# A layer of triangle multiplication and spectral convolution: the last tile's column sums by matmul, the product's bias on GpSimd

## The chip, the cores and the metric

The kernel runs on one core of a Trainium2 chip. The metric is device time in microseconds, from the start to the end of one execution; the median of three executions before the change is 1853.18 us (1850.88 to 1853.84).

Engines are named as in the profile: PE (TensorE, matmuls; PEld is its loading of weights), DVE (VectorE), ACT (ScalarE), POOL (GpSimd), SP (SyncE, which here only issues transfers). SBUF is the working memory of 128 partitions, PSUM the memory that PE writes to; POOL doesn't read PSUM in this kernel.

## What is computed

The input x is 512 x 512 positions of 64 channels, float32. Layer 0 is a gated triangle product, layer 1 a convolution in the spectral domain, each behind a group norm and added to its input. Cut to what matters:

```python
xn = _ln(x, norm_w, norm_b)                       # x is already group-normed
left  = (xn @ left_w + left_b) * mask * sigmoid(xn @ lgate_w + lgate_b)
right = (xn @ right_w + right_b) * mask * sigmoid(xn @ rgate_w + rgate_b)
out_gate = sigmoid(xn @ ogate_w + ogate_b)
out = einsum('bkjd,bkid->bijd', left, right)
out = _ln(out, onorm_w, onorm_b) @ out_w + out_b
x1 = x + out * out_gate                           # layer 0

x_ft = fft2(_gn(x1))[:, :, :12, :12]              # layer 1
out_ft = einsum('bcmn,comn->bomn', x_ft, w_real + 1j * w_imag)
x2 = x1 + real(ifft2(out_ft, padded with zeros))
```

Only 12 x 12 frequencies are kept, so that both transforms are matmuls with small tables of cosines and sines. The mask is 0 or 1 for each of the 512 rows and columns; positions whose row or column is masked out get `out_b` for the product.

## The kernel before

Rows and columns are ranked by the mask, so that those that count come first. With at most 256 of them the function `compact` runs, and it does in these executions. Its stages, with the times of the profile: statistics of x and the compact copy (to 90 us), the projections left and right (to 400 us), the products of the 64 channels (to 666 us), the rows of the product (to 815 us), the units of layer 0's output (to 1515 us), and layer 1's small transforms and the last pass (to the end).

From 666 to 1515 us one loop runs over steps s (line 1096 on), under a manual schedule: instructions stand on each engine in the order of the program, and nothing is reordered. A step is 8 positions of each of the 128 partitions; 8 steps make a tile k of 64. The first 8 tiles (`first`) are the product, held in `places`; then come 32 units v = k - 8, each a pair of 32-column tiles of x for half of the rows. `last` is unit 31. In step (k, n) PE transposes step s + 13 (`t_ps`, line 957, `LEAD` = 13), multiplies step s + 12 for its centered values (`y_ps` for the product, whose second half is already the output projection, `c_ps` for x), and ACT squares these and copies; DVE adds up the squares (L1000), ACT takes the square root (L1006) once for a tile, DVE the reciprocal of it (L1164), and DVE then multiplies the projection by that factor (L1170) into `z_t`, 16 positions in two steps, and adds a bias (L1173) that lies in PSUM (`bias_ps`, part of `scratch`). In the product `z_t` goes to DRAM as `u_d`, from SP. `z_t` has four buffers, `xt_c` 15.

In the units z becomes the output gate by a sigmoid on ACT (L1124); POOL multiplies it by the product's rows that `load_u` brought from `u_d`, or by the bias row where the row is masked (`gated`, L1026), and adds it to x in place (`added`, L1030). The result is stored to `x_h` by SP (`store`), measured for the group norm by DVE (L1075), and reduced over rows by PE into `f_ps` (`transform`, L1057), 24 sums for each of 32 columns. `save` copies `f_ps` to `ft` and writes it to DRAM, `modes_d`, one row for each of the 512 columns. A quarter of these, 128 columns, is brought back with columns as partitions (`fetch`) and summed over columns by 12 matmuls (`column_sums`, L891), which DVE adds to `sums` (L894). The first three quarters are summed inside the loop (`columns`, at the units 11, 19 and 27). The last needs the last unit: after the loop `fetch(3)` runs on POOL's queue, behind `memset` of `picks`, and its matmuls stand among the steps of the group norm's affine (`group_norm_affine`, whose argument `between` is called after its two matmuls).

`sums` are then turned (L1227), scaled into `picks`, multiplied by the weights (`mixed_ps`, L1245), and transformed back for the first columns (`back_columns`). The last pass takes 64 tiles of 128 rows and 32 columns (1024 KB each): four matmuls (`l_ps`, L1309), four adds on DVE (L1316), a store to the output. These tiles are gathers from `x_h` on POOL (`fetch_rows`, line 914), in rank order, with 15 buffers (`AHEAD`): two are fetched inside the loop, at step n = 3 of the last two units, 11 after `fetch(3)`, two into `picks` when the mixing is done, and each of the others when a tile has left its buffer. `load` (line 1008) brings the units' x tiles, also by gathers on POOL, and is called at n = 3 and 6 three units ahead. Everything on POOL, gathers too, keeps its order.

`places` is one SBUF tensor of eight parts (`place(i)`): the product, then x of five units at a time (`x_of`: parts 0, 1, 3, 4, 2), `u` in parts 5 and 6, `modes_t` and `ft` in part 7, and at the end the weights from part 3 on.

Of the kernel before, what the change touches and what calls it, by code (L numbers as in the profile page):

```python
# [9 lines left out]
F32 = mybir.dt.float32  # L10
# [36 lines left out]
def conv_preact_kernel(ctx: ExitStack, tc: tile.TileContext, t: dict):  # L47
# [193 lines left out]
    def group_norm_affine(keep, sets, each, name, between=lambda i: None):  # L241
# [5 lines left out]
        with tc.tile_pool(name="gn_" + name, bufs=1) as gp, tc.tile_pool(  # L247
# [6 lines left out]
            between(0)  # L254
# [12 lines left out]
            between(1)  # L267
# [346 lines left out]
    def compact(fc):  # L614
# [193 lines left out]
        with tc.tile_pool(name="tri", bufs=1) as trp:  # L808
# [57 lines left out]
            with tc.manual_schedule(), tc.tile_pool(name="late", bufs=1) as lp:  # L866
# [4 lines left out]
                nc.scalar.dma_start(turn, t["c_turn"])  # L871
                sums = lp.tile([P, MODES, M2], F32, name="sums")
# [12 lines left out]
                def column_sums(h, pool):  # L885

                    by = modes_t.rearrange("p (m k) c -> p m (k c)", k=2)
                    ps = pool.tile([P, 4, P], F32, name="t_ps").rearrange("p i k -> p (i k)")[:, : MODES * M2]
                    ps = ps.rearrange("p (m n) -> p m n", m=MODES)
                    steps = [  # L890
                        lambda m=m: nc.tensor.matmul(ps[:, m, :], by[:, m, :], col_basis[:, h, :], start=True, stop=True)  # L891
                        for m in range(MODES)
                    ]
                    return steps + [lambda: nc.vector.tensor_add(sums, sums, ps)]  # L894

                def columns(h, pool):
                    for step in column_sums(h, pool):
                        step()

                def fetch(h):  # L900

                    (nc.gpsimd if h == 3 else nc.sync).dma_start(modes_t, modes_d[h * P : (h + 1) * P])
# [4 lines left out]
                buffers = [places[:, free : free + JC * C].rearrange("p (n c) -> p n c", c=C)]  # L907
                buffers += [place(i)[:, r * JC : (r + 1) * JC] for i in (6, 2, 0, 1) for r in range(2)]
                buffers += [place(7)[:, JC:]]
# [8 lines left out]

                with tc.tile_pool(name="np_x", bufs=LEAD + 2) as tp, tc.tile_pool(
# [5 lines left out]
                ) as s1, tc.tile_pool(name="np_t", bufs=2, space=PSUM) as ps_t, tc.tile_pool(  # L925
                    name="np_n", bufs=1, space=PSUM
                ) as ps_n, tc.tile_pool(name="opf", bufs=1, space=PSUM) as ps_f, ExitStack() as products:
# [14 lines left out]
                    totals = [scratch[:, i, : SIZE * 8] for i in range(2)]  # L942
                    eps = lp.tile([P, 1], F32, name="eps")
# [119 lines left out]
                    def save(jc):  # L1063
                        ft = places[:, 7 * 64 * C + M2 * C : 7 * 64 * C + 32 * C].rearrange("p (j c) -> p j c", c=C)
                        nc.scalar.copy(ft.rearrange("p j c -> p (j c)"), fs.pop(jc))
                        for g in range(4):
                            o = jc * JC + 8 * g
                            queue = nc.scalar if jc == NJ - 1 else nc.sync
                            queue.dma_start(modes_d[o : o + 8].rearrange("j m c -> m j c"), ft[32 * g : 32 * g + M2])
# [29 lines left out]
                    for s in range(-LEAD, total_g + 2 * SIZE):  # L1099
# [49 lines left out]
                        if (v, n) in ((last - 1, 3), (last, 3)):  # L1149
                            fetch_rows(len(fetched))  # L1150

# [11 lines left out]
                        if n == 7 and k + 1 in rss:  # L1163
                            nc.vector.reciprocal(rss[k + 1], rss[k + 1])  # L1164
                        if wps is not None:
# [3 lines left out]
                            rs = rss[k][:, 8 * n : 8 * n + 8].unsqueeze(2).to_broadcast([P, 8, C])  # L1169
                            nc.vector.tensor_mul(z[:, 8 * odd : 8 * odd + 8, :], wps, rs)  # L1170
                            if odd:
                                bias = bias_ps["out" if k < first else "ogate"]
                                nc.vector.tensor_add(z, z, bias.unsqueeze(1).to_broadcast([P, 16, C]))  # L1173
# [21 lines left out]
                        if n == 6 and v % 8 == 3 and 8 < v < len(units):  # L1195
                            columns(v // 8 - 1, ps_t)
                        if v == last - 1 and n == 3:
# [3 lines left out]
                with tc.tile_pool(name="lq", bufs=1) as qp, tc.tile_pool(name="lx", bufs=1) as xp:  # L1201

                    picks = qp.tile([P, MODES, MODES, 32], F32, name="picks")
                    nc.gpsimd.memset(picks, 0.0)
                    fetch(3)
                    buffers += [xp.tile([P, JC, C], F32, name=f"lx_t{i}") for i in range(AHEAD - 2 - len(buffers))]
                    spare = picks.rearrange("p m n k -> p (m n k)")
                    buffers += [spare[:, i * JC * C : (i + 1) * JC * C].rearrange("p (n c) -> p n c", c=C) for i in range(2)]
# [6 lines left out]
                    with tc.tile_pool(name="tcp", bufs=1, space=PSUM) as tcp:  # L1215
                        steps = column_sums(3, tcp)

                        def some(i):
                            for step in steps[7 * i : 7 * i + 7 - 2 * i]:
                                step()  # L1220

                        ab2 = group_norm_affine(lp, sets, 8, "x1c", some)
                        steps[-1]()
                    with tc.tile_pool(name="sps", bufs=1, space=PSUM) as sps:

                        turned = sps.tile([P, MODES, M2], F32, name="turned")
                        nc.tensor.matmul(  # L1227
                            turned.rearrange("p m n -> p (m n)"), turn, sums.rearrange("p m n -> p (m n)"), start=True, stop=True
                        )
# [28 lines left out]


# [137 lines left out]
```

## Time and profile before

The profiled execution took 1856.55 us, its span of instructions is 1854.8 us; both lie near the three of the median.

| stretch, us | PE | DVE | ACT | POOL | clock | GB/s |
|---|---|---|---|---|---|---|
| whole span, share | 89% | 78% | 51% | 47% | 0.89 | 252 |
| product, 690 to 785 (95 us) | 88 | 91 | 79 | 3 | 0.96 | 167 |
| units, 900 to 1000 (100 us) | 97 | 98 | 74 | 96 | 0.98 | 262 |
| 1500 to 1550 (50 us) | 23 | 30 | 4 | 29 | 0.59 | 352 |
| last pass, 1600 to 1700 (100 us) | 91 | 69 | 12 | 20 | 0.50 | 426 |

The numbers of the engines are busy microseconds of the stretch. The clock is the share of full speed that PE was granted. [...] GB/s is what the transfers moved. In the groups of instructions, a row gives line, engine, operation, tile written and read, shapes and count, then busy time, mean of one in ns, and the idle time of the engine just before them with what ended it. PE's float32 matmuls leave two records each. In the chain of waits, a row is a start, a length and the engine and line that held the end at that time; the letters q stand for the queue of an engine that issues a transfer.

### The profile page before, as it was taken

The page shows a single profiled execution, that of the slowest core. Times are in us where ns is not written, and L with a number is a line of the kernel's source. Part 1 is how long each engine was busy: PE and PEld are TensorE (multiplying, and loading weights), DVE is VectorE, ACT ScalarE, POOL GpSimd, SP SyncE. Part 2 cuts the span into 40 slices and gives each one's busy share as a digit, 9 for nine tenths or more (in the row PEclk, how much of TensorE's full clock was granted, in tenths as well). Part 3 has the DMA queues.
Part 4 walks back from the last instruction along what each step waited for, and adds up shares of the span by engine and source line. Part 5 has one row for each costly group of instructions (what it writes and reads, how often), then busy time and mean ns, then how long its engine had stood idle before and what let it go on. Part 6 is the DMA issues. An engine that isn't in the chain of part 4 may idle for free.

```text
span 1854.8 us, 33850 instructions
## 1 busy us (share of the span) xinstructions
PE 1644.3 (89%) x11598; PEld 1295.3 (70%) x11598; DVE 1455.1 (78%) x3001; ACT 952.9 (51%) x1670; POOL 873.7 (47%) x678
## 2 busy tenths in 40 slices
PE   6779899999899999989999999999999957998772
PEld 5666666664688777788888888888888736665441
DVE  5989677777455559999999999999999984665552
ACT  3555555554222268877777767777777720111000
POOL 3666111111000000039999999999999882112110
PEclk9989899999899999999999999999999966555555
DMA  6999255556655525347767776687676598999998
GB/s 250 383 384 374 83 130 138 139 140 159 202 181 181 177 100 199 137 159 249 259 236 244 264 272 215 230 306 248 232 264 242 197 275 357 408 426 426 426 427 378
DMA packets 188869, 468.23 MB, mean 252 GB/s; under 512 B 35184, under 2 KB 134384, under 8 KB 147600
## 3 DMA queue, kind: packets, MB, share of 16 engines
q1 hardware_dynamic: 158192, 262.40, 41.7%
q0 software_dynamic: 27856, 202.19, 28.5%
q8 instruction: 94, 1.54, 0.3%
q10 hardware_dynamic: 2640, 1.38, 0.3%
q14 instruction: 87, 0.71, 0.1%
HBM read 278.13 MB, written 187.76 MB: 251 GB/s over the span
## 4 chain that ended last, share of the span: by engine, by line
PE 23%; DVE 22%; DMA 8%; POOL 5%; issue 3%; ACT 2%; SPq 1%; DVEq 0%; ACTq 0%; POOLq 0%
DVE scratch L1000 5%; DVE z_t L1170 5%; DVE z_t L1173 5%; PE w_ps L967 5%; PE l_ps L1309 5%; PE c_ps L967 5%; DVE stats2c L1075 4%; DMA places<-x_h,dst_i 4%; POOL z_t L1026 3%; PE t_ps L957 3%; DMA out_x<-places 2%; PE f_ps L1057 2%; POOL places L1030 2%; PE y_ps L978 1%; DMA picks<-x_h,dst_i 1%
## 5 line engine op out<-in xcount | busy, mean ns | idle before, releaser
L967 PE MATMUL w_ps<-gate_x,xt_c 128*128 128x128 f32 x2048 | 282.7, 282 | 31.1 <-DVE z_t L1170 29.5
L1030 POOL TENSOR_TENSOR places<-places,z_t 128x1024 f32<-128x1024 f32 x127 | 302.2, 2379 | 8.1
L967 PEld LDWEIGHTS w_ps<-gate_x,xt_c 128*128 128x128 f32 x2048 | 254.4, 195 | 47.5 <-DVE z_t L1170 45.6
L967 PE MATMUL c_ps<-center_x,xt_c 128*128 128x128 f32 x2048 | 277.9, 279 | 6.1 <-ACT xt_c L962 5.5
L967 PEld LDWEIGHTS c_ps<-center_x,xt_c 128*128 128x128 f32 x2048 | 253.5, 195 | 9.8 <-ACT xt_c L962 8.2
L1309 PE MATMUL l_ps<-places,rinv 24*128 24x512 f32 x512 | 206.7, 1128 | 29.2 <-DVE places L1316 18.0
L1075 DVE BATCH_NORM_STATS2 stats2c<-places 128x6 f32<-128x128 f32 x1024 | 220.4, 278 | 8.2 <-POOL places L1030 8.2
L1000 DVE TENSOR_REDUCE scratch<-sq_c 128x16 f32<-128x1024 f32 x160 | 194.5, 1216 | 21.7 <-ACT sq_c L995 7.6
L1124 ACT ACTIVATE z_t<-z_t 128x1024 f32<-128x1024 f32 x128 | 135.5, 1058 | 141.9 <-DVE z_t L1173 126.3
L1173 DVE TENSOR_TENSOR z_t<-z_t,scratch 128x1024 f32<-128x1024 f32 x160 | 195.3, 1221 | 11.6 <-ACT rs_n L1006 3.8
L957 PE MATMUL t_ps<-c_ident,places 128*128 128x128 f32 x1280 | 200.4, 280 | 1.3 <-DVE places L855 1.3
L1309 PEld LDWEIGHTS l_ps<-places,rinv 24*128 24x128 f32 x512 | 120.9, 304 | 110.0 <-DVE places L1316 54.1
L1026 POOL TENSOR_TENSOR z_t<-z_t,bias_row_out 128x1024 f32<-128x1024 f32 x63 | 149.6, 2374 | 100.0 <-ACT z_t L1124 99.7
L957 PEld LDWEIGHTS t_ps<-c_ident,places 128*128 128x128 f32 x1280 | 145.6, 142 | 60.7 <-issue 51.5
L630 POOL DMA_INDIRECT places<-in_x,src_i x64 | 62.6, 978 | 258.5 <-PE t_ps L957 246.9
L962 ACT ACTIVATE xt_c<-t_ps,ab_xc 128x512 f32<-128x512 f32 x256 | 175.9, 687 | 15.5 <-PE t_ps L957 10.2
L1170 DVE TENSOR_TENSOR z_t<-w_ps,rs_n 128x512 f32<-128x512 f32 x256 | 171.8, 672 | 5.3 <-PE w_ps L967 5.3
L1316 DVE TENSOR_TENSOR places<-places,l_ps 128x512 f32<-128x512 f32 x176 | 109.3, 682 | 79.3 <-PE l_ps L1309 39.8
L992 ACT ACTIVATE sq_c<-c_ps 128x512 f32<-128x512 f32 x256 | 150.5, 588 | 31.0 <-PE c_ps L967 30.7
L680 DVE BATCH_NORM_STATS2 stats1c<-x_ps 128x6 f32<-128x512 f32 x256 | 155.7, 680 | 12.4 <-PE x_ps L679 12.0
L1026 POOL TENSOR_TENSOR z_t<-z_t,places 128x1024 f32<-128x1024 f32 x64 | 151.5, 2367 | 15.1 <-ACT z_t L1124 15.0
L665 ACT COPY xc<-xg 128x128 f32 x352 | 105.0, 298 | 68.3 <-POOL xc L665 32.5
(208 smaller groups left out, 2614.7 us busy)
## 6 DMA issues: line engine op xcount, KB each, us to landing
x_h<-places SPq DMA_DIRECT2D x64, 1024.0 KB
out_x<-places SPq DMA_DIRECT2D x44, 1024.0 KB
places<-u_d SPq DMA_DIRECT2D x512, 64.0 KB
left_d<-o_c SPq DMA_DIRECT2D x64, 256.0 KB
right_d<-o_c SPq DMA_DIRECT2D x64, 256.0 KB
left_raw<-left_d SPq DMA_DIRECT2D x64, 256.0 KB
right_raw<-right_d SPq DMA_DIRECT2D x64, 256.0 KB
u_d<-z_t SPq DMA_DIRECT2D x32, 512.0 KB
```

Source lines behind the costliest of these rows:

```text
L680: nc.vector.bn_stats(stats[:, 0, 16 * (jc % quarter) + 4 * r + c, :], ps.rearrange("p i k -> p (i k)"))
L957: nc.tensor.transpose(tps[:, i, :], flat[:, o : o + P], ident)
L962: nc.scalar.activation(xts[s], tps, AF.Identity, bias=ab1[:, 2:3])
L967: nc.tensor.matmul(ps[:, 2 * i : 2 * i + 2, :], xts[s][:, i, :], w, start=True, stop=True)
L992: nc.scalar.activation(sq, cps, AF.Square)
L1000: nc.vector.tensor_reduce(totals[k % 2][:, 8 * (n - 1) : 8 * (n + 1)], sqs.pop(s // 2), AX.X, ALU.add)
L1026: nc.gpsimd.tensor_mul(zs[k, c], zs[k, c], u)
L1030: nc.gpsimd.tensor_add(xr, xr, zs.pop((k, c)))
L1075: nc.vector.bn_stats(st[k // 4][:, g, k % 4, :], x_of(k)[:, :, 2 * g : 2 * g + 2])
L1170: nc.vector.tensor_mul(z[:, 8 * odd : 8 * odd + 8, :], wps, rs)
L1173: nc.vector.tensor_add(z, z, bias.unsqueeze(1).to_broadcast([P, 16, C]))
L1309: nc.tensor.matmul(ps.rearrange("p j o -> p (j o)"), rinv[h, b, :], it[h], start=True, stop=True, tile_position=(32 * g, 0),)
```

## The change

Four things are changed.

1. In the product the bias of `z_t` is added by POOL from the row in SBUF, and no longer by DVE. The units keep theirs on DVE.
2. In the product the reciprocal is written to two halves of `scratch` in PSUM (`factors`), and the multiplication reads it there. DVE's inputs are then one from SBUF and one from PSUM.
3. The last quarter of the columns is split. Its first 96 columns are fetched at (last, 5) from ACT's queue and multiplied at (last, 7) into `t_ps`, 12 matmuls that start an accumulation. The last 32 columns don't go through DRAM: 16 matmuls multiply `ft`, as it stands in SBUF, by `spread_e` and add to the same `t_ps`. `spread_e` holds the cosines and sines of these 32 columns, spread over 12 x 24 places so that each row of `ft` reaches its own; ACT builds it in 24 instructions of 192 elements from two new constants (`last_basis`, `last_mask`) in steps 2 to 5 of the last unit, in a part of `places` that the last `u` has left. `sums` takes `t_ps` between the variance's matmul and the root, where `turned` is now issued too.
4. The order of the last pass's buffers is changed, and one gather more is issued in the loop (at (last - 2, 3)) and one directly after it, ahead of the `memset`.

On POOL the six gathers of the first three units, which were its first instructions in this stage, now stand among the adds of the product: the first after 21 of them, the others two adds apart.

```diff
-    def group_norm_affine(keep, sets, each, name, between=lambda i: None):
+    def group_norm_affine(keep, sets, each, name, between=lambda: None):
...
             nc.tensor.matmul(mean_ps, avg, part, start=True, stop=True)
-            between(0)
...
             nc.tensor.matmul(var_ps, avg, v, start=True, stop=True)
-            between(1)
+            between()
...
+                last_basis = lp.tile([P, 8, M2], F32, name="last_basis")
+                nc.scalar.dma_start(last_basis, t["c_last_basis"])
+                last_mask = lp.tile([P, M2], F32, name="last_mask")
+                nc.scalar.dma_start(last_mask, t["c_last_mask"])
...
+                def columns(h, pool):
+                    q = P if h < 3 else P - JC
...
+                    for m in range(MODES):
+                        nc.tensor.matmul(ps[:, m, :], by[:q, m, :], col_basis[:q, h, :], start=h < 3 or m == 0, stop=h < 3)
+                    if h < 3:
+                        nc.vector.tensor_add(sums, sums, ps)
+                    return ps
...
-                    (nc.gpsimd if h == 3 else nc.sync).dma_start(modes_t, modes_d[h * P : (h + 1) * P])
+                    q = P if h < 3 else P - JC
+                    (nc.scalar if h == 3 else nc.sync).dma_start(modes_t[:q], modes_d[h * P : h * P + q])
+                spread_e = places[:, 7 * 64 * C - 8 * 2 * MODES * M2 : 7 * 64 * C]
+                spread_e = spread_e.rearrange("p (j k m n) -> p j k m n", j=8, k=2, m=MODES)
+                def prepare(some):
+                    for i in some:
+                        nc.scalar.mul(spread_e[:, :, i // MODES, i % MODES, :], last_basis, last_mask[:, i : i + 1])
...
-                buffers = [places[:, free : free + JC * C].rearrange("p (n c) -> p n c", c=C)]
-                buffers += [place(i)[:, r * JC : (r + 1) * JC] for i in (6, 2, 0, 1) for r in range(2)]
-                buffers += [place(7)[:, JC:]]
+                buffers = [place(7)[:, JC:], places[:, free : free + JC * C].rearrange("p (n c) -> p n c", c=C)]
+                buffers += [place(2)[:, r * JC : (r + 1) * JC] for r in range(2)]
...
+                    factors = [scratch[:, i, SIZE * 8 :] for i in range(2)]
...
                         nc.scalar.copy(ft.rearrange("p j c -> p (j c)"), fs.pop(jc))
+                        if jc == NJ - 1:
+                            ps = ends[0].rearrange("p m n -> p (m n)")
+                            for j in range(8):
+                                for k in range(2):
+                                    e = spread_e[:, j, k].rearrange("p m n -> p (m n)")
+                                    nc.tensor.matmul(
+                                        ps[k * C : (k + 1) * C], ft[:, j, :], e,
+                                        start=False, stop=(j == 7), tile_position=(0, k * C),
+                                    )
+                            return
...
-                        if (v, n) in ((last - 1, 3), (last, 3)):
+                        if (v, n) in ((last - 2, 3), (last - 1, 3), (last, 3)):
                             fetch_rows(len(fetched))
+                        if v == last and 2 <= n < 6:
+                            prepare(range(6 * n - 12, 6 * n - 6))
...
-                            nc.vector.reciprocal(rss[k + 1], rss[k + 1])
+                            nc.vector.reciprocal(factors[(k + 1) % 2] if k + 1 < first else rss[k + 1], rss[k + 1])
...
-                            rs = rss[k][:, 8 * n : 8 * n + 8].unsqueeze(2).to_broadcast([P, 8, C])
+                            rs = (factors[k % 2] if k < first else rss[k])[:, 8 * n : 8 * n + 8]
+                            rs = rs.unsqueeze(2).to_broadcast([P, 8, C])
...
-                                bias = bias_ps["out" if k < first else "ogate"]
-                                nc.vector.tensor_add(z, z, bias.unsqueeze(1).to_broadcast([P, 16, C]))
+                                if k < first:
+                                    bias = rows_of["out"].unsqueeze(1).to_broadcast([P, 16, C])
+                                    nc.gpsimd.tensor_add(z, z, bias)
+                                else:
+                                    nc.vector.tensor_add(z, z, bias_ps["ogate"].unsqueeze(1).to_broadcast([P, 16, C]))
...
+                        if (v, n) == (last, 5):
+                            fetch(3)
+                        if (v, n) == (last, 7):
+                            ends.append(columns(3, ps_t))
...
+                    fetch_rows(len(fetched))
                     nc.gpsimd.memset(picks, 0.0)
-                    fetch(3)
...
-                        def some(i):
-                            for step in steps[7 * i : 7 * i + 7 - 2 * i]:
-                                step()
-                        ab2 = group_norm_affine(lp, sets, 8, "x1c", some)
-                        steps[-1]()
...
+                        def turn_sums():
+                            nc.vector.tensor_add(sums, sums, ends[0])
+                            nc.tensor.matmul(
+                                turned.rearrange("p m n -> p (m n)"), turn, sums.rearrange("p m n -> p (m n)"),
+                                start=True, stop=True,
+                            )
+                        ab2 = group_norm_affine(lp, sets, 8, "x1c", turn_sums)
```

## The prediction

> **What bounds the kernel now.** I read the 40 slices first, then the groups of instructions by shape inside the stages that the change touches, then the busy time in chosen stretches, and last the chain of waits from 1500 us on. Three stages matter: the product (666 to 815 us), the units (815 to 1515 us), and the end. In the groups between 700 and 780 us (columns: line, engine, operation, tile, shapes, count, busy us, mean ns, idle before):
>
> ```profile
> L978 PE MATMUL y_ps<-both,xt_y 64*128 64x128 f32 x670 | 50.7, 293 | 6.9 <-ACT xt_y L960 6.9
> L1170 DVE TENSOR_TENSOR z_t<-xt_c,rs_n 128x512 f32<-128x512 f32 x41 | 26.4, 675 | 0.0
> L1000 DVE TENSOR_REDUCE scratch<-sq_c 128x16 f32<-128x1024 f32 x21 | 25.8, 1228 | 2.2
> L1173 DVE TENSOR_TENSOR z_t<-z_t,scratch 128x1024 f32<-128x1024 f32 x21 | 25.6, 1221 | 1.1
> L1164 DVE RECIPROCAL rs_n<-rs_n 128x64 f32<-128x64 f32 x6 | 3.3, 544 | 0.0
> ```
>
> DVE's four groups sum to 81 us, while busy overlaps a little, in 80 us: DVE is the bound of the product. It takes one pair of steps in 3.8 us plus the reciprocal's 0.54 every fourth pair: its root instructions on ACT stand at 728.88 and 744.47 us, 15.6 us for 8 steps. Between such stalls PE starts its y_ps at 735.57, 737.25, 738.92 and 740.60 us, so PE alone needs 1.68 us a step, 13.4 for 8. The stretches (us of PE, PEld, DVE, ACT, POOL, then clock, DMA share, GB/s) show that POOL has nothing to do there, and that in the units DVE and POOL are both full:
>
> ```profile
> 690.00:785.00 95.00, 88.11 (x1015) 72.78 (x1016) 90.89 (x105) 79.33 (x159) 2.81 (x3) 0.96 0.43 167
> 900.00:1000.00 100.00, 96.84 (x814) 85.88 (x813) 98.26 (x232) 73.67 (x111) 96.33 (x47) 0.98 0.75 262
> ```
>
> At the end the chain (start us, length, what) leaves the last POOL add, and goes twice through DRAM before the last column sums:
>
> ```profile
> 1514.55 2.03 PE f_ps L1057 x8
> 1516.65 0.59 ACT places L1065
> ...
> 1518.74 4.96 DMA modes_d<-places
> 1523.70 0.43 issue
> 1524.13 6.30 DMA places<-modes_d
> 1530.43 0.04 issue
> 1530.48 3.18 PE t_ps L891 x14
> 1533.66 0.46 PE var_ps L266 x2
> ...
> 1539.76 1.33 PE turned L1227 x2
> 1541.09 1.57 issue
> 1542.66 5.05 PE mixed_ps L1245 x166
> ```
>
> After it the last stage is transfers alone: the first store is issued at 1566.32, and from 1600 us on the queues move 424 GB/s with the DMA share at its full 1.01.
>
> ```profile
> 1530.00:1536.00 6.00, 5.52 (x26) 5.52 (x26) 1.59 (x9) 0.00 (x0) 4.58 (x5) 0.50 1.00 418
> 1566.00:1600.00 34.00, 29.82 (x102) 20.44 (x100) 20.73 (x34) 6.68 (x8) 4.68 (x5) 0.50 0.94 363
> 1600.00:1850.00 250.00, 191.16 (x500) 114.80 (x496) 136.01 (x220) 13.35 (x16) 41.21 (x44) 0.50 1.01 424
> ```
>
> 64 stores and the 49 gathers beyond the 15 fetched ahead, 1.05 MB each, are 118.5 MB, 280 us at 424 GB/s: 1566.3 + 280 is 1846 against a span of 1854.8. All 15 had landed by about 1562 (DMA idles between 1564 and 1566). So the end follows the first store one for one while those 15 stay early.
>
> **The product's bias and factors: -20 us.** Removed from DVE: 32 adds of 1.22 us. A pair costs it 1.23 + 2 x 0.64 = 2.5 us, a block of four with reciprocal 10.6. Next in line is PE: the 1.68 us a step while products are transposed (steps 0 to 51 of the scaling), then 1.33 us a step when the x tiles replace them (t_ps starts 1.33 us apart at 797.45 and 798.78). ACT needs 3 x 0.47 = 1.4 us a step, and a root did not delay PE at 697.72, where DVE was not yet behind. Before: the first scaling starts at 689.69, the first of the units (step 64) at 814.71, 125.0 us. After: 51 x 1.68 + 13 x 1.35 = 103.2. Gain 21.8; I keep 1.8 back for the edges, where the POOL add makes the last u_d store 2.5 us later and load_u waits for it (POOL first uses what load_u brings at 839.81, 22 us after load_u's start).
>
> Added to POOL: 32 adds, 2.37 us each by the same shape at L1026, one per pair of 3.36 (later 2.7) us. [...] on DVE the add makes the pair 3.9 us with its share of the reciprocal, on POOL it makes POOL's pair 2.4, and PE's 3.36 decides. [...]
>
> [...] With the factors left in SBUF a pair would be at least 2.37 + 1.28 = 3.65 us, a gain of only about 0.26 x 32 = 8 us. The change puts them in PSUM. The trace has no DVE instruction of that kind next to POOL before; the nearest row is L1170 in the units, one PSUM and one SBUF input, 671 ns with POOL 96% busy. [...]
>
> Two things move on POOL. The six gathers of the first three x tiles stood alone at its head and were held by PE only (670.98 to about 720 us). Now each stands behind the adds, 8 steps before its transposes: issued at about 762 (step 43's place plus DVE's and POOL's lag), wanted at 772. It has some 9 us; 1.05 MB beside u_d's stores (0.52 MB per 3.36 us, 156 GB/s) at 427 GB/s takes 4 us and some 2 to 4 to start. No stall is my value; the other end is 16.4 us landing, as the chain shows in the saturated last stage, about 7 us late once, with the following gathers spreading to 10 in all. z_t has four buffers: scaling 1.3, add 2.4, store about 4.5 make 8.2 us, against four pairs of 2.7 us at the tightest, so DVE doesn't wait.
>
> ACT's two new constant loads cost 2 x 0.63 us at the start (rows at 662.36 and 663.01); ACT's first copy there waits for PE until 666.64. Nothing.
>
> **The last tile's sums: -7 us.** Removed: the 4.96 us store, the 6.30 us fetch, the issues between, and 24 small matmul records (12 matmuls) from the path after the last f_ps. Added, in PE's order:
>
> - fetch(3), 96 rows, from ACT behind the second dozen of the 24 builds. A build has 192 elements; 64 take 0.31 us and 256 take 0.54 at L1006 and L1086, so about 0.47 us; ACT's 0.60 us instructions start 0.47 apart, so 0.34 apart here: 4 us a dozen. The first dozen fits between the sigmoids at 1495.87 and 1502.00; the second ends at 1507, and delays the next sigmoid (1505.99) by 2 us, still before POOL is free for it (1509.71). They wait for POOL's last gate from u, done at 1496.73. The fetch is issued at 1507.4 and lands after 4 to 7 us; I take 1513.
> - The 12 column matmuls are ahead of both last transforms in PE's queue: 24 records x 0.227 us (L891 at clock 0.50) = 5.45, to 1518.5. **New wait:** eight f_ps matmuls stand behind them; formerly the first four were done early and the last at 1516.6. Now 2 x 2.06 us cold gives 1522, the copy 1522.7.
> - 16 matmuls of 288 columns, two column groups at a time as f_ps has four: 8 x 288/512 of an f_ps turn, 9.3 us at the 2.06 of clock 0.50, 4.8 us at the 1.06 seen at 1447.08. [...] 5.5 of 6 us busy with small matmuls, clock 0.50 throughout. But at 1458 to 1462 dense f_ps brought it back within 4 us. [...] by the small-matmul row never, 1532; I take the dense row: 1527.6.
> - mean_ps is behind these: 1527.6 instead of 1524.82, +2.8. From there the rows give 2.7 us to v, 0.8 for var_ps, 2.8 to the affine's end, 1.4 of picks, and the add of the sums and the turn now run beside them: mixed_ps at +7.8, 1535.5 instead of 1542.66.
>
> Gain 7 (10 if the clock is full, limited by mean_ps; 0 if the fetch lands at 1516 and PE stays cold). Four tiles instead of two are fetched before the memset, and POOL no longer waits 5.8 us for modes_d, so the 15 tiles are in before 1553, ahead of the first store at 1559. The extra gather at POOL, 1 us, falls into its pauses of 1.9 and 2.6 us near 1460 and 1467.
>
> **Sum:** 20 + 7 = 27 us: span 1827.8; the profiled execution of 1856.55 becomes 1829.5, and the median 1853.18, 3.4 below it, 1826.
>
> **Rivals.** Chances are for cases, each with its time.
>
> - Forecast, both gains: 1826 (own range 1820 to 1832), 0.60.
> - Only the product gains (0.19): the fetch lands late beside the x_h stores (DMA share 1.0 from 1508 on) and the spread runs cold; mixed_ps stays at 1542. 1853 - 20 = 1833. For it: everything at the end runs at clock 0.50.
> - The product is held by its transfers (0.15): u_d stores and gathers together need about 390 of 427 GB/s in its last 28 us, gathers land late, 10 of the 20 are lost: 1836.
> - Slower (0.04): [...] A pair is then 2.37 + 1.28 + 1.23 = 4.9 us, plus reciprocals 5.0 against 3.9, 32 x 1.1 = 35 us lost, the end gains 7: 1881. [...] Against it: 98 and 96% of DVE and POOL in the same 100 us.
> - No change (0.02): PE's step turns out as long as DVE's was, and the end as in the second case: 1853.
>
> A measurement here tells changes over about 0.2%, 3.7 us. Faster 0.94, same 0.02, slower 0.04. The range takes 23 + 10 below and 12 + 0 above: 1820 to 1841.
>
> **What would show it.** Right: y_ps starts 1.68 us apart throughout, DVE about 75% busy between 690 and 770, POOL at 2.37 us an add, the units starting near 794; mixed_ps 7 us earlier relative to the last POOL add. Wrong: PE waiting for places<-in_x near 772, scalings over 0.7 us, t_ps of the column sums after 1516 on this clock, or a last stage that lengthens by what came before it.

## The result, and the profile after

The changed kernel takes 1838.98 us in the median of four runs (1835.84 to 1841.17), the kernel before 1852.22 beside it. The ratio is 0.9927, with a 95% interval of 0.9909 to 0.9944. Timed a second time, on another chip, it was 0.9937 (0.9924 to 0.9951). So the change is worth 12 to 13 us, where 27 were forecast. The profiled execution took 1835.84 us, the fastest of its four, and that of before 1856.55, slower than its median; profile against profile the difference is 20.7 us, some 7 too many. Times are therefore compared below as ratios to the kernel before on the same chip, and traces from landmark to landmark.

The groups of instructions by shape of the changed kernel, 700 to 780 us:

```profile
L1198 POOL TENSOR_TENSOR z_t<-z_t,bias_row_out 128x1024 f32<-128x1024 f32 x25 | 59.1, 2364 | 20.8 <-DVE z_t L1194 17.0 <-issue 3.1 <-POOL z_t L1198 0.6
L990 PE MATMUL y_ps<-both,xt_y 64*128 64x128 f32 x688 | 50.0, 285 | 0.0
...
L1194 DVE TENSOR_TENSOR z_t<-xt_c,scratch 128x512 f32<-128x512 f32 x48 | 31.9, 686 | 7.8 <-ACT rs_n L1018 5.4
...
L1012 DVE TENSOR_REDUCE scratch<-sq_c 128x16 f32<-128x1024 f32 x24 | 29.5, 1228 | 8.1 <-ACT sq_c L1007 6.9
```

PE's y_ps have no idle time left ahead of them, while DVE now has some, waiting for ACT; the scaling kept its length (686 ns against 675), and POOL's adds take 2.36 us. The busy time in stretches (PE, PEld, DVE, ACT, POOL, then clock, DMA share, GB/s) says the same of the product, and that the last pass is transfers as before:

```profile
690.00:785.00 95.00, 94.26 (x1088) 79.79 (x1086) 76.42 (x94) 88.01 (x173) 70.37 (x33) 1.00 0.52 199
...
1600.00:1830.00 230.00, 169.26 (x443) 99.80 (x440) 118.95 (x191) 13.34 (x16) 36.52 (x39) 0.51 1.01 425
```

In the product PE is the bound, as forecast. The end is another matter. The chain of waits of the changed kernel (start, length, what):

```profile
1465.89 26.98 DMA modes_d<-places
...
1493.05 7.57 DMA places<-modes_d
1500.62 0.04 issue
1500.66 5.31 PE t_ps L896 x24
1505.98 3.35 PE f_ps L1069 x16
...
1509.40 0.59 ACT places L1077
1510.00 0.04 issue
1510.04 4.10 PE t_ps L1083 x32
...
1521.38 3.97 PE mixed_ps L1275 x121
1525.35 2.11 issue
1527.46 3.76 PE mixed_ps L1275 x121
1531.22 2.72 issue
1533.94 1.11 PE mixed_ps L1275 x26
```

It doesn't leave the last POOL add, as before's did. It leaves a write: the sums of tile 14, which the fetch reads, took 27 us to land. The timelines of SP, ACT and POOL (start, length, engine, line, what; in brackets the idle time ahead of it, and what ended it) show why, and who stood behind it:

```profile
1458.22 0.52 SPq L1230 DMA_DIRECT2D places<-in_w_real  x1
1458.79 1.38 SPq L1230 DMA_DIRECT2D places<-in_w_imag  x1
1464.66 1.62 SPq L1090 DMA_DIRECT2D modes_d<-places  x4
1468.26 31.43 SPq L1058 DMA_DIRECT2D x_h<-places  x4
...
1482.39 4.25 ACT L912 ACTIVATE places<-last_basis,last_mask 128x192 f32<-128x192 f32 x12
1493.05 0.35 ACTq L904 DMA_DIRECT2D places<-modes_d  x1
1493.44 2.00 ACT L1145 ACTIVATE z_t<-z_t 128x1024 f32<-128x1024 f32 x2 [6.81 <-DMA modes_d<-places]
...
1494.58 2.35 POOL L1038 TENSOR_TENSOR z_t<-z_t,bias_row_out 128x1024 f32<-128x1024 f32 x1 [5.36 <-ACT z_t L1145]
```

On SP's queue the write stands behind the two loads of the weights, 2304 KB each. When they landed, SP's waits tell (engine, line, what it waited for, us in total, times, longest):

```profile
SPq L1058 <- DMA places<-in_w_imag: 0.5, 1, 0.5
```

The store behind this wait went out at 1489.51, so that w_imag was in by then, if the trace names the right wait; the write was in at 1492.9. ACT keeps its order: it held the fetch until the write was in, and with it the last two sigmoids, so that POOL stood for 5.4 us. Then PE, in its order too, ran the fetched columns ahead of f_ps.

This table is worked out from the timelines of all engines. Each row is the time from one landmark to the next, in us.

| from, to | before | changed | changed, again | product alone | tail alone | write on ACT | sums behind f_ps | gathers late |
|---|---|---|---|---|---|---|---|---|
| product's first scaling to units' first w_ps | 120.0 | 103.6 | 103.6 | 103.6 | 120.0 | 103.6 | 103.6 | 103.6 |
| to the end of the last POOL add | 704.8 | 709.6 | 711.5 | 704.4 | 708.9 | 704.5 | 703.5 | 712.2 |
| to the start of mixed_ps | 28.2 | 22.0 | 23.8 | 26.7 | 22.3 | 25.0 | 22.0 | 22.5 |
| to the first store | 23.7 | 26.5 | 26.1 | 24.6 | 27.4 | 25.9 | 26.0 | 20.5 |
| to the end | 288.5 | 286.3 | 286.4 | 288.4 | 286.8 | 286.5 | 287.1 | 295.1 |
| sum | 1165.1 | 1147.9 | 1151.3 | 1147.6 | 1165.5 | 1145.4 | 1142.2 | 1153.8 |

Before against changed: the product gave 16.4 us, the units took back 4.7, the stretch behind the last add gave 6.1 (7 were forecast), and the mixing took back 2.8. The columns to the right are the experiments. Each column is one execution; the two of the changed kernel differ by up to 1.9 us in a row and by 3.4 in the sum, so that one difference of that size is no finding by itself.

### The profile page after: what moved, and what is told of

The parts are those of the page before. It is cut to its first block, busy times and chain, and to the rows that moved or that the text cites. A ratio compares the mean times of both kernels' runs of the same rounds, so it can differ in the third digit from the quotient of the medians.

```text
span 1834.1 us, 33997 instructions
## 1 busy us (share of the span) xinstructions
PE 1628.8 (89%) x11630; PEld 1286.6 (70%) x11630; DVE 1422.9 (78%) x2969; ACT 962.2 (52%) x1694; POOL 947.5 (52%) x709
## 4 chain that ended last, share of the span: by engine, by line
PE 25%; DVE 18%; DMA 12%; POOL 3%; issue 2%; ACT 2%; SPq 1%; DVEq 0%; ACTq 0%; POOLq 0%
DMA out_x<-places 8%; PE w_ps L979 5%; PE c_ps L979 5%; DVE stats2c L1096 4%; DVE z_t L1194 4%; PE t_ps L969 4%; DVE scratch L1012 4%; PE l_ps L1340 4%; PE y_ps L990 4%; DVE z_t L1200 4%; PE f_ps L1069 2%; DMA modes_d<-places 1%; POOL z_t L1038 1%; POOL places L1042 1%; DMA places<-x_h,dst_i 1%
## 5 line engine op out<-in xcount | busy, mean ns | idle before, releaser
L1198 POOL TENSOR_TENSOR z_t<-z_t,bias_row_out 128x1024 f32<-128x1024 f32 x32 | 75.7, 2364 | 245.8 <-DVE z_t L1194 241.7
L974 ACT ACTIVATE xt_c<-t_ps,ab_xc 128x512 f32<-128x512 f32 x256 | 176.2, 688 | 10.3 <-PE t_ps L969 9.3
L1200 DVE TENSOR_TENSOR z_t<-z_t,scratch 128x1024 f32<-128x1024 f32 x128 | 156.3, 1221 | 10.0 <-ACT rs_n L1018 3.8
L1038 POOL TENSOR_TENSOR z_t<-z_t,places 128x1024 f32<-128x1024 f32 x64 | 151.6, 2369 | 17.0 <-ACT z_t L1145 13.6
L1038 POOL TENSOR_TENSOR z_t<-z_t,bias_row_out 128x1024 f32<-128x1024 f32 x63 | 149.3, 2370 | 10.0 <-ACT z_t L1145 9.8
L733 POOL COPY rbc<-rq_out 128x512 f32<-128x512 f32 x64 | 38.3, 613 | 210.5 <-DVE rq_out L209 132.1
```

The lines of the kernel that those rows point to most:

```text
L974: nc.scalar.activation(xts[s], tps, AF.Identity, bias=ab1[:, 2:3])
L1038: nc.gpsimd.tensor_mul(zs[k, c], zs[k, c], u)
L1200: nc.vector.tensor_add(z, z, bias_ps["ogate"].unsqueeze(1).to_broadcast([P, 16, C]))
```

## The experiments

Each was timed in five rounds. Ratios are to the kernel before, with their 95% intervals.

| kernel | ratio | interval |
|---|---|---|
| product alone | 0.9917 | 0.9900 to 0.9933 |
| tail alone | 1.0020 | 1.0011 to 1.0029 |
| changed, write on ACT's queue | 0.9921 | 0.9905 to 0.9937 |
| changed, factors in SBUF | 0.9995 | 0.9984 to 1.0006 |
| changed, again | 0.9937 | 0.9924 to 0.9951 |
| write on ACT, sums behind f_ps | 0.9902 | 0.9886 to 0.9918 |
| the same, part of the weights one unit earlier | 0.9908 | 0.9892 to 0.9923 |
| changed, six gathers behind the mixing | 0.9943 | 0.9929 to 0.9957 |
| changed, fetch behind the last sigmoid | 0.9940 | 0.9926 to 0.9953 |
| sums behind f_ps, three gathers behind the mixing | 0.9911 | 0.9897 to 0.9924 |
| sums behind f_ps, spread split | 1.0028 | 1.0016 to 1.0039 |
| both of these | 0.9905 | 0.9890 to 0.9920 |

### Each half alone

The product alone is the kernel before with parts 1 and 2 of the change:

```diff
-                            nc.vector.reciprocal(rss[k + 1], rss[k + 1])
+                            nc.vector.reciprocal(factors[(k + 1) % 2] if k + 1 < first else rss[k + 1], rss[k + 1])
...
+                                if k < first:
+                                    nc.gpsimd.tensor_add(z, z, rows_of["out"].unsqueeze(1).to_broadcast([P, 16, C]))
```

> The kernel before with the product's part alone: bias on GpSimd, factors in PSUM. Theory now: this part is all of the gain and the new tail gives nothing net. Product 18.9 us shorter, less some 2 us lost at the units' start because the last u_d store and so load_u come later: about 1836 us, at or a little below the changed kernel's 1839. Rival, the forecast's split: both parts gain, so that without the tail some 6 to 7 us are missing against the changed kernel: about 1845.

The tail alone is the changed kernel with these lines put back to what they were.

> The changed kernel with the product's bias back on VectorE and its factors back in SBUF, so that only the last tile's sums, the buffers' order and the earlier gathers differ from before. Theory now: the path from the last POOL add to the mixing is 6.2 us shorter, but ScalarE stands behind the fetch, which waits for a write to DRAM, and the last add comes 5.4 us later: net within 1 us of before, 1851 to 1853. Rival, the forecast: 7 us gained, 1845.

Product alone: 0.9917, 15 us less than before (12 to 18), and no slower than the whole change. Tail alone: 1.0020, 3.7 us more than before (2.0 to 5.4), which is worse than either theory. **The whole gain is the product's; the new tail loses a little.** The column of tail alone shows what moved: the last add comes 4.1 us later, the mixing starts 5.8 earlier behind it, and the first store 3.8 later behind that. In these two executions the sums differ by 0.4 us only, so the table doesn't place all of the 3.7. Nor was part 4 of the change, the buffers' order and the earlier gathers, tried apart from part 3.

### Factors in SBUF

```diff
-                            nc.vector.reciprocal(factors[(k + 1) % 2] if k + 1 < first else rss[k + 1], rss[k + 1])
+                            nc.vector.reciprocal(rss[k + 1], rss[k + 1])
...
-                            rs = (factors[k % 2] if k < first else rss[k])[:, 8 * n : 8 * n + 8]
-                            rs = rs.unsqueeze(2).to_broadcast([P, 8, C])
+                            rs = rss[k][:, 8 * n : 8 * n + 8].unsqueeze(2).to_broadcast([P, 8, C])
```

> The changed kernel with the product's factors left in SBUF, so that VectorE's scaling of w_ps reads one input from PSUM and one from SBUF, as in the units. Theory of exclusion[...]: a pair is 2.37 + 1.28 = 3.65 us instead of 3.36, some 8 us longer over the product: 1847. Rival: as the units' scalings of this form show beside a busy POOL, no exclusion, the scaling stays at 0.68 us: 1839, no difference to the changed kernel. In between if GpSimd's adds lengthen a little.

The expectation misreads one thing: in the product the value that is scaled is `xt_c`, a copy in SBUF, and not w_ps in PSUM. With the factors in SBUF both of DVE's inputs are then in SBUF, which isn't the form of the units' scaling, so the rival had no ground. Timelines of DVE and POOL in this kernel:

```profile
726.59 1.21 DVE L1012 TENSOR_REDUCE scratch<-sq_c 128x16 f32<-128x1024 f32 x1
727.72 1.99 DVE L1193 TENSOR_TENSOR z_t<-xt_c,rs_n 128x512 f32<-128x512 f32 x1
729.63 0.54 DVE L1187 RECIPROCAL rs_n<-rs_n 128x64 f32<-128x64 f32 x1
730.10 0.62 DVE L1193 TENSOR_TENSOR z_t<-xt_c,rs_n 128x512 f32<-128x512 f32 x1
...
726.80 2.36 POOL L1197 TENSOR_TENSOR z_t<-z_t,bias_row_out 128x1024 f32<-128x1024 f32 x1 [1.29 <-DVE z_t L1193]
```

The scaling that starts at 727.72, beside POOL's add, takes 1.99 us and ends 0.55 us behind that add's end (729.16). The next, with POOL idle, takes 0.62, and the reduction, with one input, its 1.21 beside POOL. POOL's adds start 3.65 us apart (719.51, 723.16, 726.80), the very 2.37 + 1.28 of the prediction, an estimate of its author that no trace of before showed. From the first scaling to the first w_ps it is 115.4 us, against 103.6 with the factors in PSUM. So 11.8 of the product's 16.4 us hang on the place of 64 numbers a partition; moving the bias alone would have given 4.6.

### What holds the tail

```diff
-                            nc.sync.dma_start(modes_d[o : o + 8].rearrange("j m c -> m j c"), ft[32 * g : 32 * g + M2])
+                            queue = nc.scalar if jc == NJ - 2 else nc.sync
+                            queue.dma_start(modes_d[o : o + 8].rearrange("j m c -> m j c"), ft[32 * g : 32 * g + M2])
```

> The changed kernel with the write of tile 14's column sums (modes_d) issued from ScalarE's queue, where nothing large stands ahead of it, and no longer from SyncE's behind the weights' two loads. Theory: the write lands in about 5 us instead of 27, the fetch doesn't wait for it, ScalarE isn't held, the last sigmoids and POOL's last add come 5.4 us earlier, and with them the whole end: about 1834 us, 5 below the changed kernel. Rival: all queues share the same engines, which are full with the weights and the stores, and the write lands as late as from SyncE: 1839, no difference.

The chain of this kernel:

```profile
1484.50 15.31 DMA places<-modes_d
1499.85 5.31 PE t_ps L896 x24
1505.16 3.46 PE f_ps L1069 x16
```

The write went out at 1466.49, and the fetch was issued at 1484.50 without waiting for it. ACT wasn't held, and the last add is again 704.5 us behind the first w_ps: that the wait for the write had held the add is shown. That the order on SP's queue made the write late is shown less well, because one thing more differs here. SP issued w_real at 1460.04 but w_imag only at 1479.49, 18.9 us after the first issue had ended (why, the trace doesn't say), so that the write had one load beside it and not two. w_real took 16.4 us from issue to landing. The fetch now took 15 us itself, with a DMA share of 1.12 in the mean from 1480 to 1490. It landed 708.5 us behind the first w_ps, only 2.3 earlier than in the changed kernel, and f_ps still stood behind it. In time (0.9921) this can't be told from the change. The other way round, only the fetch and its matmuls were moved, behind the last sigmoid:

```diff
-                        if (v, n) == (last, 5):
+                        if (v, n) == (last + 1, 0):
                             fetch(3)
-                        if (v, n) == (last, 7):
                             ends.append(columns(3, ps_t))
```

> The changed kernel with nothing but the place of the fetch and of the 12 column matmuls moved: behind the last sigmoid on ScalarE, and behind the first half of the last transform on PE. Tile 14's write stays on SyncE's queue. Theory: the fetch can't start before the write has landed, so it starts when it did; ScalarE is no longer held, and POOL's last add comes 5 us earlier, but PE takes the fetched columns first and the last half of f_ps behind them: mean_ps only 1 to 2 us earlier, 1 to 2 us gained in all, ratio to before 0.992 to 0.993. Rival: ScalarE's wait alone is what the new tail loses; then all 5 us come back: ratio 0.990 to 0.991.

ACT wasn't held here either: the last add is 705.7 us behind the first w_ps, 3.9 less than in the change. The time is still that of the change (0.9940). The rival is out: ACT's wait alone is not what the tail loses. What is left is the fetch's late landing and PE's order behind it, so the column matmuls were put behind the last f_ps, with the write on ACT's queue as above:

```diff
                         if jc == NJ - 1:
+                            ends.append(columns(3, ps_t))
...
-                        if (v, n) == (last, 7):
-                            ends.append(columns(3, ps_t))
```

> The changed kernel with tile 14's write from ScalarE's queue, and with the 12 column matmuls of the 96 columns issued behind the last transforms (f_ps) instead of ahead of them: f_ps and its copy then run while the fetch is still under way. Theory: in the changed kernel f_ps stands behind a fetch that lands at about 1500 us whatever queue the write takes, and with f_ps the copy on ScalarE and the statistics behind that copy; freed of it, mean_ps comes some 4 us earlier: 1831 to 1832 against 1835 to 1836 with the write alone. Rival: what ends last is the fetch itself and the spread behind it, which doesn't move, or the transfers of the last pass: no difference, 1835 to 1836.

PE's timeline in this kernel:

```profile
1496.42 1.94 PE L1069 MATMUL f_ps<-places,hb 128*32 128x512 f32 x8 [3.69 <-POOL places L1042]
1499.42 5.31 PE L896 MATMUL t_ps<-col_basis,places 96*128 96x24 f32 x24 [1.06 <-DMA places<-modes_d]
1504.67 6.48 PE L1084 MATMUL t_ps<-places 128*64 128x288 f32 x32
1511.07 0.41 PE L253 MATMUL mean_ps<-part,c_avg_p 128*128 128x32 f32 x2
```

f_ps and its copy ran while the fetch was under way, and PE then waited for it only 1 us. The ratio is 0.9902, 0.35% (6.5 us) under the change timed on the same chip, whose interval it doesn't touch. Two edits made this gain together; the order on PE was not timed without the write's move, and the write alone (0.9921, on another chip) has an interval that overlaps. The traces give the order its part: from the units' first w_ps to mixed_ps it is 725.5 us here, 729.5 with the write alone and 731.6 in the changed kernel. The ratio is the lowest of this study, but it can't be told from product alone (0.9917, on another chip): that the mended tail gains anything over no new tail is not shown by time. The spread took 6.5 us here and 4.1 in the changed kernel; the granted clock was 0.55 in the mean from 1505 to 1510 and 1.00 from 1510 to 1515 here, and 1.00 over the whole spread there.

The next kernel loaded 28 of the weights' 64 output channels one unit earlier.

```diff
-                        if v == last - 1 and n == 3:
+                        if (v, n) in ((last - 2, 6), (last - 1, 3)):
+                            h = slice(0, 28) if v == last - 2 else slice(28, C)
...
```

> The same with 28 of the weights' 64 output channels loaded one unit earlier (the part of SBUF that unit 27 has left), so that fewer of their 576-byte pieces are under way when the fetch is issued. Theory: the fetch took 15 us because the transfer engines were full of these pieces and of the stores; with about half of them gone it lands in 8 to 10 us, before the last POOL add, and the end moves by up to another 2 us: 1829 to 1831. Rival: it is the stores and the gathers that fill the engines then, and the weights' pieces are in either way: no difference to the run before it in this list.

No difference (0.9908). (The expectation's 576-byte pieces are not what the weights come in: among the packets of the changed kernel from 1458 to 1493 us the trace counts none between 512 bytes and 2 KB.) The columns now followed f_ps with no wait, so the fetch had landed within 13.2 us of its issue, but it was no longer what came last: DVE read mean_ps 2.4 us after PE had written it, which the chain puts down to a queue that it can't name.

### The gaps in the mixing

In the changed kernel the 288 records of mixed_ps take 13.6 us from first to last, in the tail alone 13.3; in the kernel before 10.3, and in the product alone 10.0. The gaps are "issue", time in which PE waits for nothing that the profile shows. The transfer engines are full in both kinds (DMA share 1.0 when the mixing starts). In the kernel before there is one gap behind the first record, in the changed kernel (the chain above) there are two:

```profile
1542.66 5.05 PE L1245 MATMUL mixed_ps<-places,picks 128*32 128x64 f32 x170 [1.57 <-issue]
1549.43 3.51 PE L1245 MATMUL mixed_ps<-places,picks 128*32 128x64 f32 x118 [1.72 <-issue]
```

So the second gap, and not fuller engines, is what the mixing grew by. What would the gaps be without transfers?

```diff
-                    for i in range(len(fetched), AHEAD - 2):
+                    for i in range(len(fetched), AHEAD - 8):
...
-                        for i in range(AHEAD - 2, AHEAD):
+                        for i in (AHEAD - 2, AHEAD - 1, *range(AHEAD - 8, AHEAD - 2)):
```

> The changed kernel with six of the eleven gathers ahead of the last pass issued behind the mixing instead of ahead of it, so that the transfer engines are not full while mixed_ps runs. Theory: mixed_ps takes 13.4 to 13.7 us with the new tail and 10.4 to 10.7 with the old[...]: then it takes about 10 us or less here and its gaps of 2 us and more shrink, while the six gathers, 15 us of transfers, go into the engines' idle time between 1530 and 1550: 1836 to 1840. Rival: the gaps have another cause and stay; then the end is later by what the six gathers no longer use, up to 8 us: 1843 to 1847.

PE's timeline and the busy time of this kernel, and then the busy time of the changed kernel over its mixing (the second timing):

```profile
1527.71 8.22 PE L1275 MATMUL mixed_ps<-places,picks 128*32 128x64 f32 x288 [3.24 <-issue]
...
1527.00:1536.00 9.00, 8.22 (x288) 7.98 (x288) 0.57 (x3) 0.00 (x0) 0.00 (x0) 0.86 0.02 6
```

```profile
1528.00:1542.00 14.00, 8.78 (x288) 8.03 (x288) 1.08 (x7) 0.00 (x0) 0.00 (x0) 0.70 0.72 294
```

With the transfers at rest (share 0.02) there is no gap at all: 8.2 us. (The kernel with the spread split, below, has 8.3 us without a gap, behind PE's wait of 25.8 us for transfers.) In the kernel before, in both timings of the changed kernel, with the write on ACT and with sums behind f_ps the share is 1.00 to 1.04 when the mixing starts, and each has at least one gap. So these traces have the gaps only with transfers under way; what PE waits for in them no record shows. In both timings of the changed kernel they stand behind the same records, the 132nd and the 260th, but their lengths vary with the run: 2.1 and 2.7 us in the first timing, 2.3 and 1.6 in the second, and 0.5 and 2.2 in the kernel with sums behind f_ps. Why the new tail has a second one late in the mixing was not shown.

The first store came 6.9 us earlier behind the last add than in the change's second timing (43.0 against 49.9 us), and the time didn't improve (0.9943): the last pass took 295 us instead of 286. The six tiles have to come in some time, and the transfer engines stood idle from 1525 to 1535 (share 0.01 to 0.02).

Two attempts at a middle way, on the kernel with ratio 0.9902: three gathers behind the mixing, and half of the spread behind mean_ps.

```diff
+                            spread(range(4))
+                            ends.append(lambda: spread(range(4, 8)))
...
             nc.tensor.matmul(mean_ps, avg, part, start=True, stop=True)
+            behind_mean()
```

> The version with the write on ScalarE's queue and the column matmuls behind f_ps (ratio 0.9902), with three of the gathers ahead of the last pass issued behind the mixing. Theory: the engines of the transfers fall free 7 us earlier, in the second half of mixed_ps, one of its two large gaps goes, and the first store is 2 to 3 us earlier; the last pass gives part of it back, since three tiles are still to come: 0 to 2 us gained, ratio 0.989 to 0.990. Rival: every transfer put off lengthens the end by its own length, less the 5 us that the engines stood idle ahead of the first store: 2 us lost, ratio 0.991.

The mixing took 10.7 us with one gap of 2.1, instead of 12.9, the first store came 1.3 us earlier behind the last add, and the time didn't change: 0.9911 can't be told from 0.9902, and theory and rival not from each other.

> The version with ratio 0.9902, with the second half of the 16 spread matmuls issued behind mean_ps. Theory: the sums over the partitions are ready for mean_ps at 1506.7 in that version's trace and it runs at 1511.1, behind the spread; split, VectorE's 2 us of centering run beside the second half and the end comes 2 us earlier: ratio 0.989. Rival: the first store follows the mixing, but the transfers set the end: no difference, 0.990.

In this kernel the second half of the spread stands, in program order, behind the two gathers that reuse the place of spread_e. It waited for them, and multiplied the rows of x that they had brought, so that its output is wrong. PE's waits:

```profile
PE t_ps L1087 <- DMA places<-x_h,dst_i: 25.8, 1, 25.8
```

Its 1.0028 is the price of that wait, and says nothing of the split. The last kernel has both edits, and there these gathers are among the three behind the mixing:

> Both of these together: 2 to 4 us less than the version with ratio 0.9902, if both theories hold: 0.988 to 0.989. Rival: transfers set the end, 0.990 to 0.991.

0.9905, no difference to 0.9902. mean_ps ran behind the first half, but in this trace the fetch landed later (the columns start at 1501.92), and two gaps of 2.2 and 2.5 us were there.

## Why the prediction was right, and where it was not

The time on record was 1826 with a range to 1841; 1839 came out. It is in the range because the cases in which part of the gain is lost (1833, 1836) were counted in. The forecast's own range, 1820 to 1832, misses it: that the number fits is owed to this margin, and so to luck, and not to the account of the tail. Of the two gains only the product's happened. That is the rival "only the product gains" in outcome, but not in its reasons: the fetch was late through a write ahead of it, and the spread didn't run at a clock of 0.50 throughout.

**Product, -20 us: right in mechanism, 3 to 4 us too large (by the times, 15 us with an interval of 12 to 18, it is 5 too large).** PE's steps, DVE's 76 of 95 us busy and POOL's 2.36 us an add are as told. From first scaling to the units' first scaling it is 106.1 us (686.23 to 792.33), 18.9 less than before, where 105 was said. But this mark was badly chosen. Before, the units' first scaling stood 5.0 us behind their first w_ps, because DVE was late; after, it stands 2.5 behind it. In both kernels (product alone) the last add follows the first w_ps by 704 us. So DVE's lateness was not on the path, and the gain is 16.4, the whole of what product alone then showed. load_u did come later, and POOL waited 3.2 us for u_d at 828.10, where no wait was forecast; the units made this up.

**The slower add and the place of the factors.** The adds take 2.36 us on POOL, where they took 1.22 on DVE, and PE decided, as said. With the factors in PSUM the scalings took 686 ns beside POOL's adds; with them in SBUF a pair took 3.65 us. That the latter would leave some 8 us of gain was too much: 4.6. The prediction set 3.65 us a pair without the reciprocal against 3.9 with its share. The adds behind the reciprocals stand at 715.87 and 730.85 with the factors in SBUF, 15.0 us for four pairs, where before it was 15.6.

**No stall from the x gathers: right.** PE has no wait for places<-in_x; the nine gathers issued from 757.6 to 821.5 landed within 5.6 to 8.2 us.

**Last tile, -7 us: wrong; the tail alone costs 3.7 us.** The step that failed is "The fetch is issued at 1507.4 and lands after 4 to 7 us". It took the fetch to wait for ACT's builds alone. The fetch also reads what tile 14's write brings, and that write was on SP's queue behind the weights; before, nothing read it until 39 us later (1485.18 to 1524.13). The trace of before had the answer, in SP's waits:

```profile
SPq L1046 <- DMA modes_d<-places: 3.6, 1, 3.6
```

The store behind this wait went out at 1512.78: the same write, issued from 1485.18 to 1486.8, was in only then, some 26 us later, as in the changed kernel. From this step followed a second error, that the sigmoid would be 2 us late and still early enough: it waited 6.8, and POOL 5.4. The landing is not only a matter of this wait, since without it (write on ACT) the fetch itself took 15 us, where 4 to 7 were said.

**From the last add to the mixing, 7 us less: 6.1, right in number by luck.** The last add had itself come 4.7 us later, through the same wait, so that the stretch behind it looks shorter. Where the add isn't held (write on ACT) it is 25.0, 3.2 less than before. Counted from the units' first w_ps, mixed_ps starts after 733.0 us before, 731.1 in product alone, 731.2 in tail alone, and 731.6 and 735.3 in the two traces of the changed kernel: no gain beyond what two traces of one kernel differ by. And "mixed_ps 7 us earlier" took the mixing's length as given. It grew from 10.3 to 13.6 us, by a second gap. This term was not in the sum.

**The clock.** The spread was put at 4.9 us, close to the 4.8 of a full clock. The traces have 4.1, 5.9, 6.5 and 7.1 us for it (changed, changed again, sums behind f_ps, fetch behind the last sigmoid). The granted clock was 1.00 over the whole spread in the first; in the second 0.56 in the mean from 1515 to 1520 and 1.00 from 1520 to 1525, and in the third 0.55 from 1505 to 1510 and 1.00 from 1510 to 1515. The 9.3 us of clock 0.50 throughout are in none of them. The prediction's two rows for the clock differ in what PE ran. In the kernel before, under dense matmuls and with PE busy throughout, it was 0.50 from 1459 to 1462 and 1.00 from 1463 to 1470. With sums behind f_ps PE is busy without a gap from 1499.42 on, first with the column matmuls, and the clock is 0.50 from 1500 to 1505 and 0.55 in the mean over the next 5 us. Here the row of small matmuls was the better basis.

**The end follows the first store: right, with its condition.** It is 286 to 289 us in all kernels of the table but one, and 295 where six of the 15 tiles were not fetched ahead. (The loop stands at line 1099 of the kernel before, not at 1096.)

## What to carry to other kernels

When a read is moved earlier, look at what it reads: the last write ahead of it, on which queue it stands and behind which transfers, and what stands behind the read on its own engine. Measure the gain from a point that the read can't move: most of the 6 us by which the stretch behind the last add became shorter was the add coming later. A wait holds what stands behind it on its engine (here ACT's for the write held the sigmoid 6.8 us, and POOL 5.4 behind it), so a long fetch goes behind the work that doesn't need it, on the queue's side and on PE's. An element-wise add may well go to the engine that is slower at it (2.36 us against 1.22) when that is idle, but look at what runs beside it: with a DVE scaling of two SBUF inputs there, the gain was 4.6 us instead of 16.4.

## What was not expected of the hardware

In the kernel with the factors in SBUF, a DVE scaling with two inputs from SBUF that started beside a POOL add ended 0.55 us behind the add, and took 1.99 us instead of 0.62, while a reduction with one input ran at its 1.21. With full transfer engines at their start (DMA share 1.0), 288 small matmuls took 10.3 to 13.6 us, with gaps of up to 2.7; with the engines at rest (share 0.02) they took 8.2 without a gap. In the kernel with sums behind f_ps, PE was busy without a pause from 1499.42 to 1510, and the granted clock was 0.50 from 1500 to 1505 and 0.55 in the mean from 1505 to 1510. And a write of 4 times 48 KB took 27 us behind 4608 KB of weights on the same queue; a fetch of 576 KB from a queue with nothing large in it still took 15 us beside one of the weights' loads.
